# Attention blocks as four 64x64 tiles of TensorE, scores and values in turn, with the last image's outputs after its last block

## The chip, the cores and the metric

One core of one Trainium2 chip. The metric is the device time of one launch in microseconds (us), median of several runs. With one core there is no second die to compare; where a kernel ran several times its runs agreed within 0.21% and count as fast runs. Inputs and outputs are float32 throughout.

## The reference, cut to what matters

```python
B, C, H, W = 4, 384, 48, 48;  N = H * W = 2304;  nh, hd = 8, 48
local = depthwise_conv_7x7(x)                      # then batch norm
x_norm = layernorm(x_flat)
q, k, v = split(x_norm @ qkv_w.T + qkv_b)          # per head
q = q + layernorm(local)
attn = softmax(q @ k.T * hd ** -0.5)               # 2304 x 2304 for each of 4 x 8 heads
out = x_flat + (attn @ v) @ proj_w.T + proj_b
```

Four images; in each, attention over 2304 positions for 8 heads of 48 channels. The kernel takes the queries in six groups of 384 columns (G), the heads in four pairs, the keys in 18 blocks of 128: 4 x 6 x 4 x 18 = 1728 blocks, where a block is "128 keys, two heads, 384 queries". VectorE does most of the convolution, in the background: one instruction for each of 49 taps and three channel chunks.

## The kernel before: the parts that matter

```python
ps_r = tile_pool(bufs=3, space=PSUM)   # r:  [128, 2, 512], two banks each, a ring of three
ps_o = tile_pool(bufs=1, space=PSUM)   # o:  one bank, the sums of a pair of heads
ps_m = tile_pool(bufs=1, space=PSUM)   # m:  one bank, for means and output products

def scores(t, s):                       # a slot: six blocks (BATCH) of one pair p
    for kb in range(k0, k0 + BATCH):
        r = ring()
        for j in range(2):              # two heads, on rows 0..47 and 64..111
            rows = slice(64 * j, 64 * j + HD)
            nc.tensor.matmul(r[:, j, :G], lhsT=kk[:, blk * P : (blk + 1) * P], rhs=qq, ...)
        pt = work.tile([P, 2, G], tag="pt", bufs=9)
        nc.scalar.activation(pt, r[:, :, :G], AF.Exp, scale=SCALE)
        ... # after the third block: pair_end(), the sums of a finished pair go to SBUF

def weigh():                            # the six blocks of the slot before
    for kb, pt in batch:
        for j in range(2):              # HA = 49: 48 channels and a column of ones
            nc.tensor.matmul(sums[64 * j : 64 * j + HA, :G],
                             lhsT=values[...][:, kb % NB, 2 * p + j, :], rhs=pt[:, j, :],
                             start=kb == 0, stop=kb == KB - 1)

# a slot:  scores(t, s);  half of its taps;  weigh();  the other half of its taps
```

A score matmul contracts 48 rows and fills 128 columns of the array; the two heads lie on the two halves of the rows. A value matmul contracts 128 rows and fills 49 columns; the two heads lie on two halves of the columns. The sum of the exponentials comes as the 49th column; the reciprocals go to DRAM and back to be spread over partitions (`divide`), and multiply the group. In the last image the output products of a group are done in three slots of the next group (`OUT_SLOTS`), and the last group has an end of its own. In images 1 to 3 a finished group is stored in DRAM (`hold`) and fetched (`fetch`) while the next image's keys are made.

## Time and profile before

2971.41 us, median of three runs (2969.78 to 2972.08). Stages, read from the starts of the first score and the last value of each image in TensorE's timeline of the kernel before (us):

| Stage | Length |
|---|---|
| Setup | 149.8 |
| Attention, first image | 595.6 |
| Attention, second and third image | 585.3 each |
| Keys and values of the next image, outputs of the last (three stages) | 139.5 each |
| Last image: 72 slots with 15 output products, then the end | 618.4 + 17.1 |

The prediction below shows the header, the chain and the timelines, and how to read them. Two facts carry it. TensorE is busy 99% of the span. And TensorE runs in *rounds*: all tiles of the array, one or two here, stream 384 columns together in about 0.32 us.

### The profile page before, as it was taken

How to read it: one execution, taken by the hardware profiler on the slowest of the kernel's cores; microseconds unless marked ns; L12 is line 12 of the kernel's file. 1: busy time of each engine (PE TensorE's matmuls, PEld its weight loads, DVE VectorE, ACT ScalarE, POOL GpSimd, SP SyncE). 2: the span in 40 equal slices, each digit the busy share in tenths (PEclk: the TensorE clock that was granted, in tenths of full speed). 3: DMA queues.
4: the chain of work that ended last, by engine and by line, in shares of the span. 5: the costliest groups of instructions: out<-in, count | busy, mean ns of one | idle time of the engine just before them, and what ended most of it. 6: DMA issues, size and time to landing. Idle time of an engine off the chain costs nothing.

```text
span 2970.4 us, 42344 instructions
## 1 busy us (share of the span) xinstructions
PE 2943.2 (99%) x15658; PEld 1358.7 (46%) x15658; DVE 2309.1 (78%) x4574; ACT 1562.4 (53%) x2365; POOL 25.0 (1%) x71
## 2 busy tenths in 40 slices
PE   8999999999999999999999999999999999999998
PEld 4544444444554444444455444444455544444443
DVE  6899999998788888778788878787778867777311
ACT  4356556566225556655523555666542455555553
POOL 2000000000000000000000000000000000000000
PEclk9999999999999999999999999999999999999999
DMA  6101111111231111111132111102113210100001
GB/s 111 30 9 30 44 39 31 41 25 33 72 94 26 30 33 31 30 35 30 28 91 74 26 35 34 33 21 43 37 35 94 50 25 16 33 27 20 17 26 30
DMA packets 102189, 116.53 MB, mean 39 GB/s; under 512 B 43330, under 2 KB 88915, under 8 KB 101972
## 3 DMA queue, kind: packets, MB, share of 16 engines
q1 hardware_dynamic: 100512, 113.56, 16.4%
q8 instruction: 125, 2.05, 0.3%
q14 instruction: 92, 0.75, 0.1%
q0 software_dynamic: 960, 0.07, 0.0%
q10 hardware_dynamic: 500, 0.11, 0.0%
HBM read 79.03 MB, written 24.09 MB: 35 GB/s over the span
## 4 chain that ended last, share of the span: by engine, by line
PE 96%; DVE 3%; DMA 1%; ACT 0%; issue 0%; ACTq 0%; SPq 0%; DVEq 0%
PE r L722 39%; PE o L737 38%; PE r L446 17%; DVE acc L243 3%; PE m L446 1%; PE m L364 0%; DMA staged<-in_qkv_wT_dram 0%; PE r L975 0%; DMA taps_in<-in_conv_w_dram 0%; PE o L261 0%; DMA vec<-natural 0%; DVE xn L372 0%; DVE sq L352 0%; DVE sq L353 0%; ACTq L165 0%
## 5 line engine op out<-in xcount | busy, mean ns | idle before, releaser
L726 ACT ACTIVATE pt<-r 128x768 f32<-128x768 f32 x1728 | 1275.7, 812 | 970.1 <-PE o L737 492.5
L243 DVE SCALAR_TENSOR_TENSOR acc<-slab,vec,acc 128x368 f32<-128x368 f32 (+5 forms) x3447 | 1747.9, 588 | 0.0
L737 PE MATMUL o<-pt,v 128*49 128x384 f32 x6912 | 1175.7, 490 | 0.1
L722 PE MATMUL r<-xn,k 48*128 48x384 f32 x5184 | 908.5, 497 | 0.0
L737 PEld LDWEIGHTS o<-pt,v 128*49 128x49 f32 x6912 | 426.6, 124 | 710.6 <-issue 663.5
L722 PEld LDWEIGHTS r<-xn,k 48*128 48x128 f32 x5184 | 438.5, 185 | 469.1 <-ACT pt L726 231.7
L722 PE MATMUL r<-qt,kt 48*128 48x384 f32 x1728 | 300.4, 494 | 0.0
L446 PE MATMUL r<-xn,w_qk 128*128 128x384 f32 x864 | 283.7, 486 | 0.0
L722 PEld LDWEIGHTS r<-qt,kt 48*128 48x128 f32 x1728 | 149.9, 185 | 150.2 <-ACT pt L726 68.6
L446 PEld LDWEIGHTS r<-xn,w_qk 128*128 128x128 f32 x864 | 164.2, 190 | 114.5
L352 DVE TENSOR_TENSOR sq<-sq 128x384 f32<-128x384 f32 x47 | 26.2, 557 | 162.4 <-ACT sq L349 162.2
L446 PE MATMUL r<-w_v,xn 128*128 128x384 f32 x432 | 144.4, 487 | 0.0
L643 DVE RECIPROCAL rd<-rd 128x24 f32<-128x24 f32 (+2 forms) x25 | 7.5, 302 | 169.3 <-DMA rd<-den 169.3
L475 ACT COPY v<-r 128x384 f32<-128x384 f32 x72 | 32.1, 481 | 200.9 <-PE r L446 200.9
L446 PEld LDWEIGHTS r<-w_v,xn 128*128 128x128 f32 x432 | 81.8, 190 | 58.2 <-issue 1.8
L700 DVE SCALAR_TENSOR_TENSOR xr<-r,pb,xr 128x384 f32<-128x384 f32 x57 | 33.3, 612 | 87.6 <-ACT xn L494 84.0
L494 ACT ACTIVATE xn<-r,qkb 128x384 f32<-128x384 f32 x72 | 41.7, 580 | 97.5 <-PE r L446 95.5
L446 PE MATMUL r<-af,w_o 128*128 128x384 f32 x270 | 89.5, 486 | 0.0
L481 ACT ACTIVATE k<-r,qkb 128x384 f32<-128x384 f32 x72 | 39.3, 580 | 57.4 <-PE r L446 57.4
L446 PEld LDWEIGHTS r<-af,w_o 128*128 128x128 f32 x270 | 51.3, 190 | 35.8
L626 ACT COPY ao<-o 49x384 f32<-49x384 f32 x141 | 66.7, 473 | 1.7
L700 DVE SCALAR_TENSOR_TENSOR xr<-m,pb,xr 128x384 f32<-128x384 f32 x15 | 9.3, 617 | 59.6 <-PE m L446 59.6
(117 smaller groups left out, 827.7 us busy)
## 6 DMA issues: line engine op xcount, KB each, us to landing
xr<-in_x_dram SPq DMA_DIRECT2D x24, 576.0 KB
out_dram<-xr SPq DMA_DIRECT2D x72, 192.0 KB
slab<-in_x_dram SPq DMA_DIRECT2D x32, 378.0 KB
xn<-in_x_dram SPq DMA_DIRECT2D x48, 216.0 KB
rb<-rden SPq DMA_DIRECT2D x48, 216.0 KB
held<-ao SPq DMA_DIRECT2D x15, 576.0 KB
af<-held SPq DMA_DIRECT2D x15, 576.0 KB
slab<-in_x_dram SPq DMA_DIRECT2D x16, 297.0 KB
```

The costliest lines, as they stand in the source:

```text
L243: nc.vector.scalar_tensor_tensor(dst, src, weight, dst, ALU.mult, ALU.add)
L352: nc.vector.tensor_add(self.buf[:, 0, :], src[:, 0, :], src[:, 1, :])
L446: nc.tensor.matmul(dst, lhsT=weights(c), rhs=src(c), start=c == 0, stop=c == CC - 1)
L475: nc.scalar.copy(v[:, blk, :, 0:HD], r[:, :C].rearrange("p (h d) -> p h d", d=HD))
L481: nc.scalar.activation(k[:, u, :], r[:, :G], AF.Identity, bias=qkb[:, 1, u : u + 1])
L494: nc.scalar.activation(src[:, i, :], q[:, :G], AF.Identity, bias=qkb[:, 0, i : i + 1])
L626: nc.scalar.copy(dst[r : r + HA], sums[r : r + HA, :G])
L643: nc.vector.reciprocal(rd, rd)
L700: nc.vector.scalar_tensor_tensor(xr[:, co, :], m, pb[:, co : co + 1], xr[:, co, :], ALU.add, ALU.add)
L722: nc.tensor.matmul(r[:, j, :G], lhsT=kk[:, blk * P : (blk + 1) * P], rhs=qq, start=True, stop=True)
L726: nc.scalar.activation(pt, r[:, :, :G], AF.Exp, scale=SCALE)
L737: nc.tensor.matmul(sums[r : r + HA, :G], lhsT=values[t // NG, kb // NB][:, kb % NB, 2 * p + j, :], rhs=pt[:, j, :], start=kb == 0, stop=kb ...
```

## The change

The intent: scores and values get the same tile shape, so that the shape never changes inside the attention. The time that TensorE loses at a change is called a drain in the texts on record, and a shape a mode; the prediction reads 0.41 us for the two changes of a slot. Each block is now four score matmuls of 48 rows (in a 64-row tile) by 64 keys, and four value matmuls of 64 keys by 64 columns (49 used). The two halves of the keys lie on different row tiles, and a value sum gets two banks of PSUM, one for each half; that one bank would not do for both is the assumption. They are added at the end of a pair: ScalarE copies one, VectorE adds the other. To find room in PSUM (both kernels use 8 banks: 6 + 1 + 1 and 4 + 4), the score ring falls from three to two and the bank `m` goes. Blocks alternate: the scores of one, then the values of the block two before (`LAG`). The output products of the last image leave the slots and come at its end, through DRAM.

```diff
-    ps_r = ... bufs=3 ;  ps_o = ... bufs=1 ;  ps_m = ... bufs=1
+    ps_r = ... bufs=2 ;  ps_o = ... bufs=2        # both of two banks
...
+    halves = [slice(64 * i, 64 * i + 64) for i in range(2)]
+    def score(t, p, kb):
...
+        for j in range(2):
+            for h in halves:
+                nc.tensor.matmul(r[h, j, :G],
+                    lhsT=kk[:, blk * P + h.start : blk * P + h.stop], rhs=qq, ...)
+        nc.scalar.activation(pt, r[:, :, :G], AF.Exp, scale=SCALE)
+        if jobs: jobs.popleft()()                 # squares, one chunk at a time
...
+    def weigh():
+        for i, h in enumerate(halves):
+            for j in range(2):
+                nc.tensor.matmul(sums[halves[j], i, :G],
+                    lhsT=values[...][h, first : first + 64], rhs=pt[h, j, :],
+                    start=kb == 0, stop=kb == KB - 1)
...
+    def attend(t, s, half):                       # three blocks
+        for kb in ...:
+            score(t, p, kb)
+            if len(weighing) > LAG: weigh()
...
+    def pair_out():  nc.scalar.copy(dst[0 : 64 + HA], sums[0 : 64 + HA, 0, :G])
+    def pair_add():  nc.vector.tensor_add(dst, sums[0 : 64 + HA, 1, :G], dst)
...
-            if s in OUT_SLOTS and g and not next_image:
-                output_step(t - 1, OUT_SLOTS.index(s))
...
+    for before in range(NT - NG, NT):             # the end: six groups
+        if last: ao = outputs[before][0];  nc.vector.tensor_mul(ao, ao, rb)
+        else:    load_residual(before + 1)
+        for co in range(CC):
+            if co % 2 == 0: r = two_banks()
+            project(r[:, co % 2, :G], ...w_o..., ao);  finish(before, co, ...)
+        if before + 2 < NT: ao = fetch(before + 1)
+        if before == NT - NG: rb = divide(NT - 1)
```

Cut: the checks of the denominators, the setup's products in the new buffers, and smaller adaptations.

## The prediction

> **What bounds the kernel now.** I read the header and the chain of waits first, to see which engine ends last, then TensorE's timeline in a steady stretch, then a table of stages, and last the waits.
>
> ```profile
> PE 2943.2 (99%) x15658; PEld 1358.7 (46%) x15658; DVE 2309.1 (78%) x4574; ACT 1562.4 (53%) x2365; POOL 25.0 (1%) x71
> ...
> PE 96%; DVE 3%; DMA 1%; ACT 0%; issue 0%; ACTq 0%; SPq 0%; DVEq 0%
> PE r L722 39%; PE o L737 38%; PE r L446 17%; DVE acc L243 3%; PE m L446 1%; PE m L364 0%; DMA staged<-in_qkv_wT_dram 0%; PE r L975 0%; DMA taps_in<-in_conv_w_dram 0%; PE o L261 0%; DMA vec<-natural 0%; DVE xn L372 0%; DVE sq L352 0%; DVE sq
> ```
>
> TensorE is the path: scores (L722) and values (L737) are 77% of the chain. Only what shortens TensorE's own sequence, or a new wait on it, can move the end. A program matmul in float32 leaves two records (6912 for 3456 matmuls on either line).
>
> ```profile
> 2355.32 4.21 PE L722 MATMUL r<-xn,k 48*128 48x384 f32 x24
> 2359.46 4.08 PE L737 MATMUL o<-pt,v 128*49 128x384 f32 x24
> 2363.47 4.21 PE L722 MATMUL r<-xn,k 48*128 48x384 f32 x24
> ```
>
> TensorE alone in the last image: a slot is one batch of scores and one of values, six blocks each, and lasts 2363.47 - 2355.32 = 8.15 us. Starts are 4.14 and 4.01 us apart.
>
> ```profile
> 1001.43 0.13 PEld L737 LDWEIGHTS o<-pt,v 128*49 128x49 f32 x2 [0.19 <-issue]
> 1001.76 0.13 PEld L737 LDWEIGHTS o<-pt,v 128*49 128x49 f32 x2 [0.19 <-issue]
> 1002.08 0.13 PEld L737 LDWEIGHTS o<-pt,v 128*49 128x49 f32 x2 [0.19 <-issue]
> 1002.40 0.13 PEld L737 LDWEIGHTS o<-pt,v 128*49 128x49 f32 x2 [0.19 <-issue]
> 1003.14 1.59 PEld L722 LDWEIGHTS r<-xn,k 48*128 48x128 f32 x12 [0.61 <-issue]
> ```
>
> The weight loads show the rhythm: a pair, one load per array tile, every 0.322 us. That is a "round": all tiles stream one pass of 384 columns together. The projections, which fill the whole array with one tile, take the same (139.52 us for 432 records, 0.323). Twelve rounds are 3.87 us, so of the slot's 8.15 us 24 x 0.3225 = 7.74 are rounds and 0.41 are lost at the two changes between shapes: the load after the last pair of values comes 0.74 us after the pair before, not 0.32.
>
> ```profile
> 150.00:254.00 104.00, 100.64 (x576) 44.12 (x576) 103.70 (x200) 58.75 (x83) 0.00 (x0) 0.97 0.11 19
> 254.00:352.00 98.00, 98.00 (x582) 42.54 (x580) 97.45 (x192) 58.00 (x84) 0.00 (x0) 1.00 0.17 40
> 352.00:449.00 97.00, 97.00 (x576) 41.85 (x574) 94.72 (x186) 58.11 (x84) 0.00 (x0) 1.00 0.14 32
> ...
> 983.00:1080.00 97.00, 97.00 (x574) 42.07 (x574) 78.59 (x155) 57.99 (x84) 0.00 (x0) 1.00 0.16 38
> 1080.00:1178.00 98.00, 98.00 (x580) 42.20 (x576) 79.74 (x157) 58.00 (x84) 0.00 (x0) 1.00 0.14 31
> ```
>
> One row for each group of twelve slots, then busy PE, PEld, DVE, ACT. In the first image (first three rows) VectorE is busy 95 to 100% of the time; in the second image (last two) about 81%. VectorE is a second bound in the first image, hidden in its 78% on average.
>
> [...] 0.41 us at two changes in each slot, and none between tiles of one shape. [...] here two tiles do so, a pair to a round. Nothing in this trace shows four. [...] The nearest the trace has is a burst of one-column matmuls:
>
> ```profile
> 174.60 2.17 PE L446 MATMUL m<-vbp,w_o 128*128 128x1 f32 x18
> ```
>
> That is 2.17 / 18 = 0.12 us for a load and a matmul, 60 ns an instruction, set perhaps by the 128-column load (190 ns mean).
>
> **The change part by part.**
>
> 1. Rounds. Before, a block (128 keys, two heads) is 2 score and 2 value matmuls on two tiles: 4 rounds. After, it is 4 and 4 on four tiles: 8 x 2 passes / 4 tiles = 2 + 2 rounds, again 4. The array was full before and is full after; the change wins no arithmetic. What goes away is the drain: scores and values have one mode. A slot goes from 8.13 us (585.4 us for the 72 of the second image, 885.07 to 1470.49 in the chain) to 6 x 4 x 0.3225 = 7.74. An image: 72 x 7.74 = 557, plus 1 for its two ends: 558. Gain 27.5 us an image if nothing else binds.
>
> 2. Weight loads. Twice as many, with 64 columns. From 124 ns at 49 columns and 185 at 128, 64 is about 136 ns (estimate); four a round fit even as two overlapping pairs, 0.27 of 0.32 us.
>
> 3. ScalarE. One exp per block, 0.812 us, as before; a block lasts 1.29 us. The score ring falls from three to two. The scores of block k need the exp of k-2: it starts about 0.2 us after those scores end, ends 1.0 us after, and the next user of the buffer starts 1.29 + 0.645 = 1.93 us after. About half a microsecond is left if the weights are to be loaded ahead. The pair's copy (0.47), once for both heads and not twice, and squares cut in three (about 0.5 each) go into the gap one at a time. I charge nothing.
>
> 4. VectorE. It adds the second bank: 96 additions of 384 columns from PSUM at about 0.58 us (an SBUF addition is 0.557, the bias addition from PSUM 0.612) = 56 us, 2.3 a group. In the second and third image 79 + 2 of 92.9 us still fits. In the first it doesn't: from one query's end to the next VectorE had 91 to 96 us of work, which becomes 93 to 98, more than TensorE's 92.9. So groups 0 to 4 gain about 2 us in all, the sixth, which needs no further query soon, about 5 to 7. I take 9 us for the first image, not 27.5.
>
> 5. The last image. Before: 2335.0 to 2970.4 = 635.4 us, of which 585.4 are the slots' own, 33 are fifteen output products in the slots (2.20 us each with their drains) and 17 the end after the last value. After: 558, then all 18 products at the end: 18 x 6 x 0.3225 = 34.8. The loads for them: a stored group (590 KB) took 2.6 us of transfer at DMA share 0.89 and about 1 us ahead of it. In the built order the fetch of the fourth group stands behind the third's second output, so I count 3 us of waiting there and 1 elsewhere, 6 for the last addition, store and judgement. End: 34.8 + 4 + 6 = 45 against 50. Last image 603; gain 32.
>
> 6. Setup (149.8) and three projection stages (139.5 each): same products, four two-bank buffers in turn for three and one. No charge.
>
> Sum: 149.8 + 587 + 3 x 139.5 + 2 x 558 + 603 = 2874. I add 8 us for ScalarE waiting on a late VectorE now that the score ring is short: 2882 us, 3.0% less than 2971.
>
> **The rivals.**
>
> A. Four tiles do not run four at a time, or issue can't feed them. Four loads and four matmuls must be issued in 0.322 us, 40 ns each, twice today's rate. At 50 ns a round is 0.40 and the attention (1728 x 4 rounds) grows by 530 us. For: nothing in the trace is issued that densely for long. Against: pairs start 6 ns apart from the queue; the two-head pairs show row tiles and column tiles each running together; and the author's own measure of VectorE's room in half a slot goes from 4.0 to 3.8, while three blocks at 1.29 are 3.87. Chance about 0.11; time 3050 to 3500.
>
> B. TensorE stays at the drainless rate but waits on ScalarE or VectorE. Before, a batch of six with three rings and nine exp tiles hid a 2 us hiccup; now half a microsecond is hidden. At 2 us a group over 24 groups: 2920, within 2%. For: first image; TensorE already stood 3.4 us on VectorE's sum in group 0. Against: VectorE has 12% to spare later, and the denominators now come a slot earlier, while VectorE idled 169 us on them in 19 waits. Chance about 0.14.
>
> C. The first image gains in full (VectorE catches up where few taps are due) and the end streams: 2855.
>
> **Range and chances.** Centre 2882; 8 in 10 between 2845 and 2945. Faster by over 2% (below 2912) 0.75, within 2% 0.13, slower 0.12.
>
> **What would show it.** Step 1: the weight loads come in fours every 0.322 us with no 0.7 us gap, TensorE's records double, and a steady image's slots take about 558 us. Step 2: score and value loads near 136 ns. Step 3: no long waits of score loads on exp in the second image. Step 4: VectorE near 100% in the first image, near 87% in the second. Step 5: about 45 us after the last value, with one wait of about 3 us on a fetched group. Wrong if a block takes clearly more than 1.29 us in the second image (A), if the waits view names exp or VectorE ahead of score loads for over 50 us (B), or if the first image shortens by 20 us or more (C).

## The result, and the profile after

2887.03 us, median of four fast runs (2884.56 to 2889.39), beside 2971.55 for the kernel before (2969.78 to 2972.08). The ratio of the two is 0.9716, with a 95% interval of 0.97 to 0.9733: faster by 2.8%, where 3.0% had been predicted. Ratios in this document are the mean time of one kernel's fast runs over that of the other's in the same rounds, so they are not quite the ratio of the medians. The output is correct.

The header of the page of the changed kernel, and the engines' part of its chain of waits:

```profile
span 2887.3 us, 70195 instructions
...
PE 2841.7 (98%) x29474; PEld 1398.5 (48%) x29474; DVE 2351.0 (81%) x4661; ACT 1649.4 (57%) x2340; POOL 21.6 (1%) x89
...
PE 89%; DVE 8%; DMA 2%; ACT 0%; issue 0%; POOL 0%; SPq 0%; ACTq 0%; DVEq 0%; POOLq 0%
```

TensorE's records went from 15658 to 29474, almost double, and its busy time *fell* by 101 us. Instruction counts are no cost here; rounds and the gaps between them are. VectorE's share of the chain grew from 3% to 8%: this is where the first image and the end are no longer bound by TensorE alone.

The weight loads in the steady stretch that the prediction shows of before, now of the changed kernel:

```profile
1000.11 0.15 PEld L730 LDWEIGHTS r<-xn,k 48*64 48x64 f32 x4 [0.17 <-issue]
1000.43 0.15 PEld L751 LDWEIGHTS o<-pt,v 64*64 64x64 f32 x4 [0.18 <-issue]
1000.75 0.15 PEld L751 LDWEIGHTS o<-pt,v 64*64 64x64 f32 x4 [0.17 <-issue]
1001.08 0.15 PEld L730 LDWEIGHTS r<-xn,k 48*64 48x64 f32 x4 [0.18 <-issue]
```

Loads come in fours, every 0.32 us, and from scores (L730) to values (L751) and back there is no longer step. Before, the load that followed a change from values to scores came 0.74 us after the pair ahead of it. A block is four such rounds, 1.29 us.

The next table has one row for each of groups 1, 2 and 5 of the first image and a group of the second (window, its length, then busy PE, PEld, DVE and ACT with their counts, POOL, granted clock, DMA share and GB/s), and, last, the end of the program after the last value:

```profile
147.00:247.00 100.00, 95.33 (x1110) 43.82 (x1110) 99.10 (x193) 60.53 (x82) 0.00 (x0) 0.97 0.10 20
247.00:341.00 94.00, 91.08 (x1108) 42.30 (x1104) 93.38 (x183) 58.71 (x80) 0.00 (x0) 0.98 0.17 42
...
534.00:627.00 93.00, 93.00 (x1156) 43.09 (x1152) 89.50 (x188) 63.18 (x88) 0.00 (x0) 1.00 0.18 37
963.00:1056.00 93.00, 93.00 (x1156) 42.85 (x1152) 80.33 (x158) 61.38 (x83) 0.00 (x0) 1.00 0.18 40
2828.60:2887.30 58.70, 41.81 (x114) 21.67 (x110) 13.82 (x26) 0.48 (x1) 0.00 (x0) 0.88 0.46 146
```

In the first two rows VectorE is busy 99% and TensorE isn't (95 and 97%): the bound has moved to VectorE. In the third TensorE is full again, and VectorE still at 96%. In the second image TensorE is full and VectorE has 14% left. The last row is the end: TensorE is busy 41.8 of 58.7 us, at a mean clock of 0.88.

By stage (us), from the same starts and ends:

| Stage | Before | Predicted | After | Gain |
|---|---|---|---|---|
| Setup | 149.8 | 149.8 | 146.4 | 3.4 |
| First image | 595.6 | 587 | 583.7 | 11.9 |
| Three projection stages | 418.6 | 418.5 | 418.8 | 0 |
| Second and third image | 1170.6 | 1116 | 1120.0 | 50.6 |
| Last image with its end | 635.5 | 603 | 559.6 + 58.8 | 17.1 |
| Reserve | | 8 | 0 | |

The gains add up to 83 us, the difference of the two profiled spans (2970.4 and 2887.3). The setup's 3.4 us say nothing: in profiles of kernels with the same new setup it took 145.8 to 150.9 us.

Waits of the score loads on the exponential in the second image, before (first line) and after (second), as total, times and longest in us:

```profile
PEld r L722 <- ACT pt L726: 74.5, 220, 0.6
```

```profile
PEld r L730 <- ACT pt L738: 1.5, 8, 0.3
```

The ring is shorter and yet waited for less. Scores now come one block at a time with a block of values between, so ScalarE has 1.29 us for its 0.81 us of work; before, six came in a row and ScalarE fell behind in each batch.

### The profile page after: what moved, and what is told of

Its sections match the earlier page's. It is cut to its first block, busy times and chain, and to the rows that moved or that the text cites.

```text
span 2887.3 us, 70195 instructions
## 1 busy us (share of the span) xinstructions
PE 2841.7 (98%) x29474; PEld 1398.5 (48%) x29474; DVE 2351.0 (81%) x4661; ACT 1649.4 (57%) x2340; POOL 21.6 (1%) x89
## 4 chain that ended last, share of the span: by engine, by line
PE 89%; DVE 8%; DMA 2%; ACT 0%; issue 0%; POOL 0%; SPq 0%; ACTq 0%; DVEq 0%; POOLq 0%
PE r L730 35%; PE o L751 35%; PE r L465 9%; PE o L465 9%; DVE acc L249 6%; DVE xr L706 0%; DMA xr<-in_x_dram 0%; DMA staged<-in_qkv_wT_dram 0%; DMA columns<-bias 0%; DVE sq L365 0%; DMA taps_in<-in_conv_w_dram 0%; PE r L376 0%; DMA xn<-in_x_dram 0%; DMA w_v<-in_qkv_wT_dram 0%; DVE sq L364 0%
## 5 line engine op out<-in xcount | busy, mean ns | idle before, releaser
L738 ACT ACTIVATE pt<-r 128x768 f32<-128x768 f32 x1728 | 1400.6, 811 | 757.7 <-PE r L730 741.7
L751 PE MATMUL o<-pt,v 64*64 64x384 f32 x13824 | 1428.2, 482 | 0.0
L730 PE MATMUL r<-xn,k 48*64 48x384 f32 x10368 | 1073.7, 483 | 10.2 <-ACT pt L738 8.2
L751 PEld LDWEIGHTS o<-pt,v 64*64 64x64 f32 x13824 | 528.0, 132 | 592.9 <-issue 588.3
L730 PEld LDWEIGHTS r<-xn,k 48*64 48x64 f32 x10368 | 395.7, 133 | 457.9 <-issue 409.2
L730 PE MATMUL r<-qt,kt 48*64 48x384 f32 x3456 | 356.3, 482 | 0.1
L730 PEld LDWEIGHTS r<-qt,kt 48*64 48x64 f32 x3456 | 130.7, 132 | 149.2 <-issue 138.7
L465 PE MATMUL o<-xn,w_qk 128*128 128x384 f32 x450 | 153.3, 486 | 0.0
L465 PE MATMUL r<-xn,w_qk 128*128 128x384 f32 x414 | 141.0, 486 | 0.0
L465 PE MATMUL o<-w_v,xn 128*128 128x384 f32 x276 | 93.4, 487 | 0.0
```

Of the source, the lines that this page charges most:

```text
L465: nc.tensor.matmul(dst, lhsT=weights(c), rhs=src(c), start=c == 0, stop=c == CC - 1)
L730: nc.tensor.matmul(r[h, j, :G], lhsT=kk[:, blk * P + h.start : blk * P + h.stop], rhs=qq, start=True, stop=True,)
L751: nc.tensor.matmul(sums[halves[j], i, :G], lhsT=values[t // NG, kb // NB][h, first : first + 64], rhs=pt[h, j, :], start=kb == 0, stop=kb ...
```

## The experiments

Twelve kernels ran, on three chips, each beside runs of the kernel before (medians there 2971.10, 2970.54 and 2970.11 us). "After" below is the changed kernel with its 2887.03 us and 0.9716. A difference between two kernels of different calls is read from the ratios and from the profile's stages.

### What does a change of shape cost, and does the order matter?

The theory: the gain is the time lost at changes of shape and nothing else. The rival: the gain comes from the new order (block by block, shorter waits), or from four tiles streaming better than two. Three kernels tell these apart. The first has the *order* of after with the *shapes* of before, so it changes shape twice a block:

```diff
-            for h in halves:
-                nc.tensor.matmul(r[h, j, :G], lhsT=kk[:, blk * P + h.start : blk * P + h.stop], ...)
+            nc.tensor.matmul(r[:, j, :G], lhsT=kk[:, blk * P : (blk + 1) * P], ...)
...
-        for i, h in enumerate(halves):
-            for j in range(2):   # four 64x64 value tiles, two banks
+        for j in range(2):
+            nc.tensor.matmul(sums[64 * j : 64 * j + HA, 0, :G],
+                lhsT=values[...][:, first : first + HA], rhs=pt[:, j, :], ...)
...
-        nc.vector.tensor_add(dst, sums[0 : 64 + HA, 1, :G], dst)   # no second bank any more
```

> The order of the changed kernel (one block of scores, one of values, in turn) with the tile shapes of the kernel before (64x128 for scores, 128x64 for values, one bank). Two mode changes a block, 1728 blocks. If the drain at a change of mode is what the change removed, each block costs the 0.41 us that a slot of the kernel before loses at its two changes: 2887 + 1728 x 0.41 = 3595 us (3500 to 3700), and the weight loads of values come 0.7 us after the scores' last. The rival, that the win comes from the order and the finer overlap of exp with TensorE and not from the shape, expects 2890 to 2930.

3455.29 us, one run, of unknown state, output correct. TensorE's timeline in the second image:

```profile
1100.28 0.92 PE L729 MATMUL r<-qt,kt 48*128 48x384 f32 x4
1101.13 0.85 PE L745 MATMUL o<-pt,v 128*49 128x384 f32 x4
1101.91 0.92 PE L729 MATMUL r<-qt,kt 48*128 48x384 f32 x4
```

A block takes 1101.91 - 1100.28 = 1.63 us, not 1.29. The attention of the second image lasts 704.1 us against 560.0: 144.1 / 432 blocks = 0.333 us for two changes. This is far outside any spread of runs, so one run is enough. The new order with the old shapes is the slowest kernel of all: the order by itself wins nothing, it multiplies the changes by six. The forecast of 3500 to 3700 us was missed on the low side, because 0.41 us for two changes was too much.

The second kernel takes two blocks of scores, then two of values, with the old shapes (the edit of the first, and):

```diff
-LAG = 2
+LAG = 3
...
             if len(weighing) > LAG:
                 weigh()
+                weigh()
```

> Tile shapes of before, but two blocks of scores and then two of values: one mode change a block, half of those of the run before. The drain theory: 2887 + 864 x 0.41 = 3241 us (3190 to 3300), on the line between the kernel before (one pair of changes to six blocks) and the alternating one. The rival (order and overlap): no more than 2930.

3161.83 us, one run, unknown state, correct; below the forecast of 3190 to 3300 for the same reason. Two blocks of scores and two of values take 2.92 us, where eight rounds take 2.59:

```profile
1100.97 1.56 PE L729 MATMUL r<-xn,k 48*128 48x384 f32 x8
1103.89 1.56 PE L729 MATMUL r<-xn,k 48*128 48x384 f32 x8
```

The image lasts 632.0 us: 72.0 / 432 = 0.167 us a block, which has one change. So one change costs 0.167 us, in both kernels. The kernel before, with two changes in each of 72 slots, lies nearly on the same line: (585.3 - 560.0) / 72 = 0.351 us for two. The 0.018 us by which that exceeds 0.333 make 1.3 us an image; no more is left for another cause, such as the score loads' waits on exponentials.

The third has the new shapes in the order of the second (only the second edit).

> The changed kernel with two blocks of scores and then two of values, all as 64x64 tiles; no change of mode, and the same 1.93 us between a block's scores and the next use of its buffer. The drain theory: the order is indifferent, 2887 us within 0.3%. The rival, that taking turns block by block is needed to hide exp: slower by 1% or more.

2887.96 us, ratio 0.9724 (0.9708 to 0.974), correct; the second image lasts 559.9 us. With one shape the order is worth nothing. The theory holds: cost goes with the *number of changes of shape*, 0.167 us each. It also explains the intent: the fine order of after, which lets the score ring be short, is affordable only with one shape.

### The first image: is VectorE the bound?

Leaving out some of the convolution's taps for the groups of the first image frees VectorE. The result is wrong (relative error 0.020).

```diff
+                if 0 < t <= NG and abs(tap // KS - PAD) == PAD:
+                    yield
+                    continue
```

> Wrong result on purpose: for the groups convolved during the first image, VectorE leaves out the taps two rows from the edge of the 7x7 window (three rows away: 14 of 49), so its work there falls by some 28%. If VectorE bounds the first image (583.7 us of attention against 560.0 in the second), the first image falls to 561 to 566 us and the whole to 2862 to 2870. The rival, that the first image is long because the short score ring stalls on exp or because of the extra products in group 0: no more than 3 us gained.

2870.24 us, ratio 0.9661 (0.9645 to 0.9678). The same groups 1 and 2 as in the table above:

```profile
147.00:247.00 100.00, 99.74 (x1195) 46.88 (x1198) 84.96 (x164) 65.34 (x88) 0.00 (x0) 1.00 0.11 21
247.00:341.00 94.00, 94.00 (x1168) 43.22 (x1164) 78.96 (x156) 61.90 (x84) 0.00 (x0) 1.00 0.19 42
```

With VectorE at 85% TensorE is full. The first image takes 564.0 us, against 583.7 in after's profile and 581.4 to 581.6 in those of four other kernels with the same first image, and the program 16.8 us less. So of the 21 to 24 us by which the first image is longer than the next ones (560.0), 17 to 20 are VectorE.

How much of that is the *new* work, the additions of the second bank? A kernel without them in the first image (wrong, relative error 0.027) tells it:

```diff
-        nc.vector.tensor_add(dst, sums[0 : 64 + HA, 1, :G], dst)
+        if t >= NG:
+            nc.vector.tensor_add(dst, sums[0 : 64 + HA, 1, :G], dst)
```

> Wrong result on purpose: in the first image alone the second bank is not added. This takes only the change's own new VectorE work out of that image, some 22 additions of 0.56 us and their gaps, 13 us. If VectorE's throughput bounds it, the first image falls from 583.7 to 570 to 575 us and the whole by 9 to 13. If the additions cost by their wait on TensorE's pairs and not by their length, or if the first image is bound by its longest chain: less than 5.

2882.7 us, ratio 0.9706 (0.9691 to 0.9721), which overlaps that of after. The first image takes 575.8 us, 5.6 to 7.9 less than in those profiles. That is below the 9 to 13 expected, though the intervals from one query's end to the next fell by some 1 to 2.2 us each. The larger part of VectorE's excess is the convolution, which was there before.

Two kernels tried to take the additions, or a tap, off VectorE. First, GpSimd adds (ScalarE copies both banks out):

```diff
         nc.scalar.copy(dst[0 : 64 + HA], sums[0 : 64 + HA, 0, :G])
+        if t < NG:
+            second = work.tile([P, G], F32, tag="second", name="second", bufs=1)
+            nc.scalar.copy(second[0 : 64 + HA], sums[0 : 64 + HA, 1, :G])
...
+        if t < NG:
+            nc.gpsimd.tensor_tensor(dst, dst, seconds.pop()[0 : 64 + HA], ALU.add)
```

> In the first image alone the second bank is copied out by ScalarE and added by GpSimd, not by VectorE. That takes 23 additions of 0.56 us = 13 us off VectorE. If VectorE bounds the first image, the whole falls by 8 to 13 us; ScalarE's extra copies (0.47 each) fit in its gaps. If the first image is bound elsewhere, or if GpSimd's additions slow VectorE down[...]: no change or slower.

2927.0 us (four runs), ratio 0.9851 (0.9835 to 0.9866), correct: 40 us *slower* than after, a clear miss. GpSimd's groups of instructions, and what was waited for in the first image:

```profile
L655 POOL TENSOR_TENSOR aot<-aot,second 113x384 f32<-113x384 f32 x6 | 85.9, 14315 | 108.8 <-ACT second L644 64.9 <-DVE acc L249 43.8
L655 POOL TENSOR_TENSOR ao<-ao,second 113x384 f32<-113x384 f32 x18 | 51.0, 2834 | 477.0 <-ACT second L644 477.0
```

```profile
PEld r L738 <- ACT pt L746: 43.6, 15, 11.9
DVE rd L675 <- DMA rd<-den: 38.3, 5, 7.9
ACT sq L359 <- DVE acc L436: 26.1, 3, 12.2
```

The same addition, 113 by 384, has a shortest record of about 1 us and a longest of 18.4; the six for a group's last pair of heads average 14.3. The waits follow from each other. The denominators come late after that addition, and VectorE stands up to 7.9 us for them, once in each of five groups. So its layer norm is late, and ScalarE's squares wait for that, up to 12.2 us. The exponentials stand behind the squares in ScalarE's queue, and the score matmuls wait up to 11.9 us on them. These last waits, of the weight loads, grew from 15.9 us in after to 43.6. The first image takes 621.7 us. Spans on GpSimd are rough in a profile, but the waits and the time are not. What makes an addition long was not shown: the 18 for the first three pairs took 1.00 to 17.1 us with a median of 1.20, the six for the last pair 1.04 to 18.4 with a median of 16.6, and no run isolates the cause. VectorE did not pay: its taps take 586 ns on average in after and 585 here.

Second, ScalarE does the first of the 49 taps for the first image's groups:

```diff
-                if tap == taps[0]:
+                if tap == taps[0] and 0 < t <= NG and n_first > 120:
+                    nc.scalar.activation(dst, src, AF.Identity,
+                                         bias=shift[:, c : c + 1], scale=weight)
+                elif tap == taps[0]:
                     nc.vector.tensor_scalar(...)
```

> The right result: in the first image the first of the 49 taps (a scale and a bias, three operations of 0.48 us a group) is done by ScalarE, which is busy 62% there. If VectorE bounds the first image, five groups fall by 1.4 us each: 5 to 8 us off the whole. If ScalarE's queue, on which TensorE waits, pays for it: no gain.

2886.03 us, ratio 0.9719 (0.9705 to 0.9732), correct: no clear difference from after, a miss. In the windows of groups 2, 3 and 4 of the first image VectorE's busy time fell by 1.0 to 1.2 us, in that of group 5 by 0.4, and in that of group 1 it stayed full. Part came back as a wait. VectorE's longest entry of waits in the stretch from 147 to 534 us, first after's, then this kernel's:

```profile
DVE sq L403 <- ACT sq L398: 0.6, 1, 0.6
```

```profile
DVE few L432 <- DMA four<-parts: 3.2, 3, 1.2
```

In after VectorE comes to the layer norm's round trip through DRAM when it has already landed; with less to do it comes earlier and waits 1.1 us each time. That can account for the lack of a gain in the groups that have such a wait. The score loads' waits on exponentials over the first image hardly changed (17.9 us in 24 waits; in after 15.9 us in 21), so they don't show ScalarE's queue paying more. Where the rest went stays open.

### The end

The end took 58.8 us where 45 was predicted (some 55 to 58.6 us in profiles of five other kernels with the same end and the new shapes). Its TensorE timeline in the changed kernel (start, length, engine, line, and in brackets what TensorE waited for):

```profile
2828.61 2.20 PE L465 MATMUL o<-af,w_o 128*128 128x384 f32 x6
2831.53 2.20 PE L465 MATMUL o<-af,w_o 128*128 128x384 f32 x6 [0.71 <-DVE xr L706]
...
2853.62 4.21 PE L465 MATMUL r<-af,w_o 128*128 128x384 f32 x6 [3.08 <-DMA af<-held]
...
2873.59 2.20 PE L465 MATMUL r<-ao,w_o 128*128 128x384 f32 x6 [1.98 <-DVE ao L985]
```

Three things are to be seen. One wait of 3.08 us on a fetched group, as predicted. A wait of about 0.7 us within every group (the second line), since the second product starts only when VectorE has read the first, though it writes the other bank of the same two-bank tile; whether the chip asks for that wait or the way the program's tiles are tracked, no run here tells apart. And two products of 4.21 us, where others take 2.10 or 2.20, after the long wait: the granted clock there was half (0.50).

```profile
2853.00:2860.00 7.00, 5.67 (x9) 2.71 (x10) 0.62 (x1) 0.00 (x0) 0.00 (x0) 0.50 0.88 299
```

In this stretch the clock was 0.50 and the DMA share 0.88: stores, a fetch and a residual's load together.

The first remedy: loads on ScalarE's queue and a group ahead, and all three products of a group before the first result is read.

```diff
-            load_residual(before + 1)
+            load_residual(before + 1, nc.scalar)
+            if before + 2 < NT:
+                coming_ao = fetch(before + 1, nc.scalar)
+        r, r2 = two_banks(), two_banks()
+        parts = r[:, 0, :G], r[:, 1, :G], r2[:, 0, :G]
+        for co in range(CC): project(parts[co], ...)
...                                                 # a check moved up
         for co in range(CC):
-            ... project(m, ...);  finish(before, co, m)
+            finish(before, co, parts[co])
```

> Only the end after the last value changes: the loads of the next group's stored attention and residual go out on ScalarE's queue, a group ahead and not behind the stores on SyncE's, and the three products of a group go to TensorE before the first is read out. If the end is 58.8 us and not 45 because loads stand behind stores and because each second product waits for VectorE's read of the first, it falls to 42 to 47 us and the whole by 12 to 16 us. The rival, that the bandwidth of the transfers bounds the end (three times 590 KB a group at about 230 GB/s is 7.7 us a group): 46 us for six groups and more, so a gain of at most 8.

The rival's 230 GB/s is an estimate: 590 KB in the 2.6 us that the prediction read for a stored group. In the end of after the transfers reached 249 GB/s from 2838 to 2846 us, at a DMA share of 0.90.

2888.54 us, ratio 0.9723 (0.971 to 0.9736), correct: no gain, a miss. The waits of 0.7 us are gone, but the waits on the fetched groups have grown:

```profile
2842.73 5.83 PE L465 MATMUL r<-af,w_o 128*128 128x384 f32 x12 [2.67 <-DMA af<-held]
2854.90 5.55 PE L465 MATMUL r<-af,w_o 128*128 128x384 f32 x12 [4.41 <-DMA af<-held]
```

The fetch was issued behind the residual's load (2837.60 after 2837.11 us, 2848.84 after 2848.35), and that load waits until the stores from its buffer have landed (in after's chain a store of 1.86 us ends at 2838.21 and the load is issued at 2838.30). The edit moved the queue without moving what it waits for. This run alone doesn't show whether bandwidth or order is the limit.

The second remedy: the outputs back into the slots, as before, but with one shape in the attention.

```diff
+            if s in OUT_SLOTS and g and not next_image:
+                m = accumulator()[:, 0, :G]
+                project(m, ...w_o..., outputs[t - 1][0]);  finish(t - 1, co, m)
...
-    for before in range(NT - NG, NT):  # six groups at the end
+    # the end: divide(NT - 1), and the last group's three products
```

> The third part of the change undone alone: the last image's outputs of groups 0 to 4 are again computed in the slots, as full-array products into the spare accumulator; only the last group's stand at the end. Each of the 15 products costs 1.94 us and two changes of mode, about 2.35, so 35 us in the slots, and the end has the chain of denominators, reciprocal, broadcast and three products, about 23. Sum 58 against 58.8: the same within 5 us. If full-array products cost no drain among 64x64 tiles: 29 + 23, faster by 6.

2896.74 us, ratio 0.9751 (0.9738 to 0.9765), correct: about 9 us slower than after. The fifteen products in the slots cost 593.9 - 559.6 = 34.3 us, 2.29 each, as expected: six rounds (1.94) and two changes of shape (0.33) make 2.27. But the end took 31.4 us, not 23, for a single group, because nothing covers the last group's denominators any more:

```profile
2878.01 1.36 DVE L994 TENSOR_TENSOR ao<-ao,rb 128x1152 f32<-128x1152 f32 x1 [6.49 <-DMA rb<-rden]
2879.47 6.41 PE L466 MATMUL r<-ao,w_o 128*128 128x384 f32 x12 [7.66 <-DVE total L1023]
```

That is what an end of six groups, as in after, is good for: the five groups' products cover the last group's round trip through DRAM. The kernel before had a special end for this (17.1 us), so that its slots and end cost 33 + 17 = 50 us, less than the 58.8 of after and less than the 65.7 here.

The tail and the GpSimd edits together:

> The two edits before this together, at both ends of the program, so they should add: 2887 less 12 to 16 and less 8 to 13, that is 2858 to 2867 us.

2924.61 us, ratio 0.9846 (0.9833 to 0.9859), correct: the loss of the one, no gain from the other.

The third remedy takes the transfers away. In the last image the query tiles of finished groups are dead, so the divided attention goes there and not to DRAM, and the six residuals are loaded into free buffers during the last group's slots. At the end only stores are left.

```diff
-                nc.vector.tensor_mul(ao, ao, rb);  hold(t - 1)
+                if next_image:
+                    nc.vector.tensor_mul(ao, ao, rb);  hold(t - 1)
+                else:
+                    kept[t - 1] = big.tile([P, CC, G], F32, tag=f"xn{g - 1}", ...)
+                    nc.vector.tensor_mul(kept[t - 1], ao, rb)
...
+            if not following and 2 <= s < 2 + NG:
+                i = s - 2
+                load_residual(t - g + i, "xr" if i < 2 else "acc" if i < 5 else "slab")
...
+    rb = divide(NT - 1)                 # first, under the five groups' products
     for before in range(NT - NG, NT):
-            ... fetch, load_residual
+            ao = kept[before]           # three products, then three finishes
```

> The run with the loads on another queue kept the end at 59 us, so its order was not the cause; what stays is the traffic itself: loads of stored attention and residual, stores, and a load that waits for a store's buffer. Here the last image's divided attention is written into the dead query tiles in place of being stored and fetched, and all six residuals are loaded during the last group into tiles that are free by then; only stores remain at the end. If traffic made the end long: 34.8 us of products and about 7 after them, 42 to 45 us against 58.8, so 2870 to 2874 us. If the end is long for another reason (VectorE's reads, the last group's denominators): 2883 or more.

2876.9 us (2874.79 to 2879.83), ratio 0.9685 (0.9672 to 0.9698), correct: **faster than both kernels**, by 3.1% than before and by about 10 us than after. The end:

```profile
2829.89 4.14 PE L465 MATMUL o<-kept,w_o 128*128 128x384 f32 x12
...
2861.49 5.83 PE L465 MATMUL r<-ao,w_o 128*128 128x384 f32 x12 [1.97 <-DVE ao L997]
```

```profile
2861.40:2867.20 5.80, 5.71 (x13) 3.17 (x14) 0.03 (x1) 0.00 (x0) 0.00 (x0) 0.71 0.06 17
```

Five groups run without a wait, 29.6 us for fifteen products. Then comes a wait of 1.97 us on the last group's division, after which the clock is 0.71 and two products take 5.83 us, not 4.03. From the last value to the end it is 48.2 us and not 58.7. Expected were 42 to 45; the rest is that slower last group, and 8 us from VectorE's last operation to the end, while the last stores land. So this end is worth about 10 us. It also has the three products ahead of the first read, which alone gained nothing (2888.54 us), and it starts the last group's division earlier. No run separates that from the transfers, but the waits on fetched groups, and the clock of 0.50 after the one of 3.08 us, are gone. The length of a wait alone doesn't decide the clock: after the wait of 1.98 us that ends at 2873.59 in after the product took the usual 2.20 us, at a clock of 1.00, and here the one after 1.97 us did not.

The last kernel has both this end and the tap on ScalarE.

> The two edits together, at both ends of the program; they touch different stages, so their gains should add: 2863 to 2868 us if both hold.

2877.1 us, ratio 0.9689 (0.9676 to 0.9702), correct: the same as with the end alone, a miss. The tap adds nothing, as when it was tried alone.

## Why the prediction was right, step by step

The predicted time was 2882 us, the measured 2887.03, within the range of 2845 to 2945 and on the predicted side of 2%. The total is nearer than its parts deserve: too-low and too-high terms nearly cancelled, which is luck.

1. **Rounds (right, the term a little too large).** The runs show that no arithmetic is won, only the time lost at changes of shape. An image takes 560.0 us where 558 was predicted, because a round is 0.3235 us on average and not 0.3225 (560.0 less 1 for the two ends, over 1728 rounds). The loss at two changes was read as 0.41 us; it is 0.35 from the stages and 0.333 from the two kernels with old shapes. Over the second and third image the gain was 50.6 us, not 55.

2. **Weight loads (right).** 132 and 133 ns for 64 columns; 136 estimated. The records are 124 ns for 49 columns and 185 to 190 for 128. All four overlap, not only pairs: four take 0.15 us in the lines above.

3. **ScalarE (right in the steady images).** No charge was due there. Score loads waited 1.5 us on exponentials in the second image, where they had waited 74.5 us. The half microsecond of slack was enough. In the first image they did wait, 15.9 us in 21 waits (4.1 in the kernel with fewer taps): that is how a late VectorE reaches TensorE through ScalarE. But those waits lie within the first image's 583.7 us, less than the 587 said, so the reserve of 8 us on top was not needed.

4. **VectorE and the first image (right in mechanism, a few us pessimistic).** Gain 11.9 us where 9 was taken. By the starts of the exponentials groups 0 to 3 gained 0.4 us together and group 4 4.3, where groups 0 to 4 were to gain about 2; the rest, some 7 us, is the last group's, of which 5 to 7 were said. VectorE was busy 99% in groups 1 and 2 and 86% in the second image, as said (near 100 and near 87). That VectorE is the bound there is shown by the kernel with fewer taps. That the new additions are its smaller part is shown by the kernel without them.

5. **The end (the term that failed).** "34.8 + 4 + 6 = 45" became 58.8. The one wait of "3 us" on a fetched group came as predicted (3.08). What the sum lacked is of two kinds. TensorE was busy 41.8 us and not 34.8: about 4 us are the two products at half clock after that wait (4.21 us each), most of the rest is that a product which no next one overlaps takes 2.20 us and not 1.94. And TensorE stood 17 us and not 10: to the 3.08 us and 6.7 after the last product come 4.4 us, about 0.7 in each of the six groups, for the read of the first product of a two-bank tile, which I had not looked for in the built order, 1.98 us for the last group's division and 0.8 us for the check of the denominators. So the end became longer than the 50 us it replaced, and the last image gained 17.1 us and not 32. The kernel with everything kept on the chip won 10 us of it back.

6. **Setup and projections (right).** 139.6 us each where 139.5 was said.

The sum of the errors in us: too low were the end by 13.8, the second and third image by 4.0, the last image's slots by 1.6 and the projections by 0.3; too high the reserve by 8, the setup by 3.4 and the first image by 3.3. That is 19.7 - 14.7 = 5.0, by which 2887 misses 2882. Rival A (four tiles don't run four at a time) is refuted: loads come in fours every 0.32 us, and the four matmuls of a round start mostly 2 to 9 ns after each other in the second image's trace. With four loads in each round of 0.3235 us too, that is 81 ns a matmul and 40 ns an instruction. Rival B (new waits on ScalarE or VectorE) is refuted for the steady images and true only in the first, where it had been counted. Rival C (the first image gains in full, the end streams) is refuted in both halves.

## What to carry to other kernels

Count the changes of tile shape on TensorE and multiply by what one costs, here 0.167 us. With four rounds a block before and after, the new tiling won only those changes, and a finer order of work is affordable only when its parts have one shape (3455.29 us with the old shapes, 2887.03 with one). When an end is moved out of a loop, add up its transfers, their order in the queue and what the buffers wait for, and the slower clock after a wait (0.50 after 3.08 us in after, 0.71 after 1.97 us in the kernel with everything kept on the chip, and 1.00 after 1.98 us in after); data that fits on the chip should stay there (the end that kept it there was about 10 us shorter). Work taken off an engine that bounds a stage is not a gain until the profile shows that the engine doesn't wait for something else instead.
